# Sums of the unit ahead: when a product with ones is made, and in which bank

## Chip, cores and metric

The kernel runs on one core of a Trainium2 chip. The metric is device time in microseconds (us). The core has five instruction streams: TensorE (PE, matrix products, with its weight loads shown as PEld), VectorE (DVE), ScalarE (ACT), GpSimd (POOL) and SyncE (SP, which here only issues DMAs). Each stream is worked off in the order in which the program wrote it, and streams wait for one another through semaphores. Products land in PSUM, which the program divides into eight banks, each 512 float32 wide on 128 partitions. An ACT or DVE instruction carries the result from there to SBUF.

## What is computed

Four cross-attention layers run one after the other on x (4 batches, 512 query rows, 256 channels), with a context of 1024 rows and 512 channels per batch. Layers 0, 2 and 3 have 16 heads of width 64 and a bias that suppresses some key columns:

```python
q = hidden_states @ Wq            # k = ctx @ Wk, v = ctx @ Wv, split into 16 heads of 64
logits = jnp.einsum('bhqd,bhkd->bhqk', q, k) * scale
logits = logits + col_bias[None, None, :, :]
probs = jax.nn.softmax(logits, axis=-1)
out = jnp.einsum('bhqk,bhkd->bhqd', probs, v)
out = out.transpose(0, 2, 1, 3).reshape(B, HW, HEADS * HEAD_DIM)
out = out @ Wo + bo
out = out + residual
```

Layer 1 has an RMS norm, 16 query heads of width 16 and 4 key heads that each serve 4 query heads ("grouped"). Everything is float32. What matters here is the softmax's denominator: for each query, the sum of exponentials over all 1024 keys.

## The kernel before

**Units and steps.** The work is cut into units of two heads for one batch: 8 units per layer and batch, 96 masked (layers 0, 2, 3) and 32 grouped (layer 1). `order()` lists 96 steps by hand. Each step has one masked unit, `g`, and some also a grouped unit, `lam`. The grouped units stand in four runs of eight steps. `coming` is the grouped unit of the next step. `by_ones` is true where a step has `lam` or `coming`: 36 steps in all. Per run these are an opening step (only `coming`), then eight with a grouped unit, where steps that prepare values (even) and steps that prepare keys (odd) take turns; in the last of them nothing is coming.

**A step** works on `g` and on the unit before it, `g1`. On PE, in the order of the program:

- `scores(g)` (lines 873 and 879): eight tiles of logits, copied by ACT to a buffer (line 883); DVE takes maxima (line 930) and later subtracts them (line 978); ACT takes exponentials (line 984); POOL adds the eight tiles to a running sum `g.acc` (line 1023).
- `attend(g1)` (line 906, 64 output columns): the exponentials of `g1`, finished in the step before, times its values, 16 matmuls.
- then a list `fill` of items, each with a planned duration: `project_out` (line 1112, output projection of two finished units), `project_q` (line 770, evacuated by ACT in line 775), `k_part` (line 556, half a product of keys; after two halves ACT copies in line 561) or `v_pair` (line 609, copied by ACT in line 616), and `attend_grouped`, which calls `attend(lam)` (line 906 with 32 columns) and copies in line 916.
- between them, from a planned time of 12 or 13 us on, `pair(i)`: the logits of the coming grouped unit (line 846, copied by ACT in line 852).

**The planner's clock.** `now` adds up the planned durations of the items. When an item returns a function (its evacuation), `pass_events(now)` first writes out all subtractions and exponentials whose due time lies below `now`, then the evacuation itself. So `now` decides how many exponentials stand ahead of an evacuation on ACT's queue. Due times: the masked unit's exponentials at 3.3 + 1.22 t (t from 0 to 7; in `by_ones` steps t = 7 comes much later), the grouped unit's at 2 t - 7.5 for t from 4 to 7 (0 to 3 stand earlier), and the masked unit's subtractions at 0.7 + 1.2 t.

**The sums.** In the 36 steps the denominators of `g1` come from PE: `sums_beside(g1)` (line 1078) multiplies `g1.acc` by a matrix of ones, two matmuls, into one bank. It returns `turned`, which is put at the head of a list `late`. `late` is worked off before the first `pair`, or at the end of the step where there is none. `turned` transposes the bank's content on DVE (line 809), takes reciprocals, transposes back, gives the bank back, and scales `g1`'s output.

**Banks.** All PSUM space is taken through `Place`. It takes the bank that was given back longest ago by the program's order, among those that are not held. In steps with grouped work (`tabled`), a single bank comes from banks 4 to 7 unless `among` says otherwise, and a double one for scores or logits from a pair of the lower banks:

```python
    if tabled[0]:
        whole = [n for n in whole if n <= last] or whole
    at = min(whole, key=lambda n: max(free[n], free[n + 1]))
elif tabled[0] and any(n in free for n in among):
    at = min((n for n in among if n in free), key=lambda n: free[n])
```

Scores use `last=4`, so they go round (0,1), (2,3), (4,5). `place_out(g1)` takes a single bank for the masked attend and holds it until `turned` is done; `place_out(lam)` takes one for the grouped attend. A bank that is taken again makes PE wait until its former content has been read.

Of the kernel before, what the change touches and what calls it, by code (L numbers as in the profile page):

```python
# [80 lines left out]
def kernel(ctx: ExitStack, tc: tile.TileContext, a: dict, out: bass.AP):  # L81
# [9 lines left out]
    def t_(shape, tag, name, bufs=1, dtype=FP):  # L91
        return sb.tile(shape, dtype, tag=tag, name=name, bufs=bufs)
# [44 lines left out]
    def give_set(g):  # L137
        sets_free.append(g.set)
# [664 lines left out]
    def reciprocal_rows(out_, in_, room):  # L803


        turned = room[:, 0:S]
        short = t_([P, S // 32, 1], "short", f"short{len(turns)}")
        turns.append(0)
        nc.vector.transpose(turned, in_)
        nc.vector.reciprocal(short, turned.rearrange("p (c r) -> p c r", r=32)[:, :, 0:1])  # L810
        nc.vector.transpose(
            out_.rearrange("p (c r) -> p c r", r=32), short.to_broadcast([P, S // 32, 32])
        )
# [78 lines left out]
    def place_out(g, width=1):  # L892
        g.place = Place(width)
        g.po, g.psum = g.place.ap[:, 0:S], g.place.ap[:, S:]

    def attend(g, blocks=range(NT)):
        for t in blocks:
            for j in range(2):
                rows = g.rows[j]
                if not g.masked:  # L900
                    rows = slice(64 * g.h + 32 * j, 64 * g.h + 32 * (j + 1))
                at, first, last = rows, 0, NT - 1
                if not g.masked:
                    at = slice(64 * (t % 2) + 32 * j, 64 * (t % 2) + 32 * (j + 1))
                    first, last = t % 2, NT - 2 + t % 2
                nc.tensor.matmul(  # L906
                    g.po[at, :], lhsT=g.v[:, t, rows], rhs=g.st[t][:, j * S : (j + 1) * S],
                    start=(t == first), stop=(t == last),
                )

    def keep_even(g):


        if g.h == 0:
            gq[g.b, "o"] = t_([P, S], "o1", f"o1_{g.name}")
        nc.scalar.copy(gq[g.b, "o"][64 * g.h : 64 * (g.h + 1), :], g.po[0:64, :])

    def keep_odd(g):
        half = gq[g.b, "o"][64 * g.h : 64 * (g.h + 1), :]
        nc.vector.tensor_tensor(half, half, g.po[64:128, :], ALU.add)  # L920
        if g.h == 0:
            g.place.back()
# [102 lines left out]
    def turn_grouped(g):  # L1025
        normalise_grouped(g, g.place.ap)
        g.place.back()
# [44 lines left out]
        scale_out(g)  # L1072

    def sums_beside(g):
        w = Place(1, among=range(8))
        m = w.ap
        for j in range(2):
            nc.tensor.matmul(  # L1078
                m[g.rows[j], :], lhsT=ones[:, 0:64], rhs=g.acc[:, j * S : (j + 1) * S],
                start=True, stop=True,  # L1080
            )

        def turned():
            g.ot = t_([P, S], "ot", f"ot_{g.name}", bufs=3)
            reciprocal_rows(g.ot, m, g.ot)
            w.back()
            scale_out(g)

        return turned

    def scale_out(g):
        nc.vector.tensor_tensor(g.ot, g.po, g.ot, ALU.mult)
        g.place.back()
# [109 lines left out]
    def head(g):  # L1203
        return steps[step_of[1, g.b, 0]][1]
# [26 lines left out]
    g0, g1 = masked[0:2]  # L1231
# [56 lines left out]
    for n in range(len(steps) + 2):  # L1288
# [4 lines left out]
        g1, attended = attended, g  # L1293
# [62 lines left out]
        late = []  # L1356
# [31 lines left out]
        by_ones = tabled[0]  # L1388
# [44 lines left out]
        def behind(add):  # L1433
            if g is not masked[-1]:
                return add
            late.append(add)

        fill, of_grouped = (
            [
                (1.8 * len(each), lambda each=each: behind(project_out(*each)))  # L1440
                for each in outs if each[0].masked == m
            ]
            for m in (True, False)
        )
# [4 lines left out]
        if fast_k:  # L1449
# [3 lines left out]
            fill = of_keys[:2] + fill + of_keys[2:4] + of_queries + of_keys[4:]  # L1453
        elif fast_v:
            of_values = fast_values(g)
            if fresh:
                of_values[1:4] = of_values[3:4] + of_values[1:3]
                fill = of_values[:2] + fill + of_grouped + of_values[2:4] + of_queries + of_values[4:]
                of_grouped = []
            else:  # L1460
                fill = of_values[:2] + fill + of_queries + of_values[2:]
# [7 lines left out]
        if lam:  # L1469

            def attend_grouped():
                while any(of is lam for _, of, _ in events):
                    events.pop(0)[2]()
                lam.v = head(lam).v
                place_out(lam)
                attend(lam)
                give_set(lam)
                late.append(lambda: keep_odd(lam))
                if lam.h == 1:
                    late.append(lambda: turn_grouped(lam))  # L1480
                return lambda: keep_even(lam)

            total, where = 0.0, 0
            while where < len(fill) and total < (8.0 if by_ones and of_values else 9.5):
                total += fill[where][0]
                where += 1
            fill.insert(where, (3.6, attend_grouped))
            if by_ones:
                fill.insert(where, (1.0, lambda: late.insert(0, sums_beside(g1))))
        elif by_ones:  # L1490
            fill.insert(2, (1.0, lambda: late.insert(0, sums_beside(g1))))
        if soon and soon.first:

            def square():
# [73 lines left out]
```

## Time and profile before

| what | value |
|---|---|
| time, median of 3 runs | 3410.82 us (3410.70 to 3411.05) |
| the profiled execution | 3411.3 us |
| its span (first to last instruction) | 3409.5 us |
| idle time of PE in front of the sums (line 1078) | 0.0 us |
| length of a key step inside a run | 36.5 us |
| length of a value step inside a run | 33.1 us |
| PE's waits on ACT's copies, longest single one | 1.1 us |

The times of the steps are counted from the end of one masked attend to the start of the next on PE's timeline. In the lines of groups, the number behind x counts records, then come busy time, mean time of one record in nanoseconds, and idle time of the engine in front of the group with what ended it. A float32 matmul leaves two records. Matmuls on different columns of the array overlap, so a group's busy time is much less than records times mean. In a timeline, a line stands for a row of instructions of one kind: start, length, engine, line, names, shapes, count, and in brackets the idle time in front of it.

### The profile page before, as it was taken

How to read it: one execution, taken by the hardware profiler on the slowest of the kernel's cores; microseconds unless marked ns; L12 is line 12 of the kernel's file. 1: busy time of each engine (PE TensorE's matmuls, PEld its weight loads, DVE VectorE, ACT ScalarE, POOL GpSimd, SP SyncE). 2: the span in 40 equal slices, each digit the busy share in tenths (PEclk: the TensorE clock that was granted, in tenths of full speed). 3: DMA queues.
4: the chain of work that ended last, by engine and by line, in shares of the span. 5: the costliest groups of instructions: out<-in, count | busy, mean ns of one | idle time of the engine just before them, and what ended most of it. 6: DMA issues, size and time to landing. Idle time of an engine off the chain costs nothing.

```text
span 3409.5 us, 42702 instructions
## 1 busy us (share of the span) xinstructions
PE 3396.9 (100%) x15520; PEld 1654.2 (49%) x15520; DVE 2956.4 (87%) x3872; ACT 2348.4 (69%) x2729; POOL 2596.1 (76%) x1337
## 2 busy tenths in 40 slices
PE   9999999999999999999999999999999999999999
PEld 5555444444444444445455454554444445454554
DVE  7888899988999889988888889888899988889887
ACT  5666688776787768876666666666678776666665
POOL 5888588875888768888668768677588888769775
PEclk9999999999999999999999999999999999999999
DMA  3232111011101120011001110011111101011100
GB/s 109 64 115 85 58 36 52 30 48 38 55 27 30 48 62 30 27 30 55 19 28 53 35 48 30 28 53 56 38 30 52 36 21 53 28 45 52 35 30 10
DMA packets 147733, 151.69 MB, mean 44 GB/s; under 512 B 23608, under 2 KB 125496, under 8 KB 147012
## 3 DMA queue, kind: packets, MB, share of 16 engines
q1 hardware_dynamic: 144958, 140.58, 13.2%
q0 software_dynamic: 2560, 8.39, 0.9%
q8 instruction: 123, 2.02, 0.3%
q14 instruction: 86, 0.70, 0.1%
q10 hardware_dynamic: 6, 0.00, 0.0%
HBM read 132.15 MB, written 15.73 MB: 43 GB/s over the span
## 4 chain that ended last, share of the span: by engine, by line
PE 92%; DVE 5%; ACT 1%; issue 1%; POOL 0%; DMA 0%; DVEq 0%; ACTq 0%; POOLq 0%
PE ps L906 21%; PE ps L669 18%; PE ps L873 18%; PE ps L556 9%; PE ps L609 9%; PE ps L1112 5%; PE ps L770 5%; PE ps L846 4%; DVE ps L890 2%; DVE st L978 1%; PE ps L1078 1%; PE ps L571 1%; ACT st L883 1%; PE ps L879 1%; PE ps L785 0%
## 5 line engine op out<-in xcount | busy, mean ns | idle before, releaser
L1023 POOL TENSOR_TENSOR st<-st 128x1024 f32<-128x1024 f32 x668 | 1581.7, 2368 | 557.1 <-ACT st L984 512.6
L984 ACT ACTIVATE st<-st 128x1024 f32<-128x1024 f32 x1024 | 1042.3, 1060 | 226.8 <-POOL st L976 117.7
L978 DVE TENSOR_TENSOR st<-st,ps 128x1024 f32<-128x1024 f32 x768 | 884.2, 1214 | 3.3
L906 PE MATMUL ps<-st,v 128*64 128x512 f32 (+1 forms) x4064 | 789.8, 595 | 0.0
L976 POOL TENSOR_TENSOR st<-st 128x1024 f32<-128x1024 f32 x256 | 597.8, 2379 | 212.0 <-DVE st L970 106.2
L883 ACT COPY st<-ps 128x1024 f32<-128x1024 f32 x768 | 713.3, 1053 | 55.6 <-PE ps L879 55.4
L890 DVE TENSOR_TENSOR ps<-ps,st 128x1024 f32<-128x1024 f32 x420 | 517.8, 1233 | 210.2 <-ACT st L883 172.1
L930 DVE TRANSPOSE_TENSOR_REDUCE tops<-st 128x32 f32<-128x1024 f32 x544 | 628.3, 1211 | 69.2 <-ACT st L852 64.5
L873 PE MATMUL ps<-qt,kt 64*128 64x512 f32 x3008 | 687.3, 596 | 0.0
L906 PEld LDWEIGHTS ps<-st,v 128*64 128x64 f32 (+1 forms) x4064 | 239.9, 130 | 535.0 <-issue 443.6
L873 PEld LDWEIGHTS ps<-qt,kt 64*128 64x128 f32 x3008 | 280.9, 186 | 345.0 <-ACT st L883 147.5
L609 PE MATMUL ps<-wv,ctx 128*128 128x256 f32 x1344 | 312.1, 385 | 1.1 <-ACT ctx L432 1.1
L669 PE MATMUL ps<-st 128*128 128x128 f32 (+1 forms) x1620 | 308.8, 339 | 2.3 <-ACT ps L692 2.1
L556 PE MATMUL ps<-ctx,wk 128*128 128x512 f32 x672 | 310.9, 604 | 0.0
L609 PEld LDWEIGHTS ps<-wv,ctx 128*128 128x128 f32 x1344 | 250.5, 190 | 92.1 <-issue 54.8
L852 ACT COPY st<-ps 128x1024 f32<-128x1024 f32 x256 | 247.0, 1018 | 62.5 <-PE ps L846 59.0
L669 PEld LDWEIGHTS ps<-st 128*128 128x128 f32 x1620 | 214.6, 192 | 94.2 <-issue 86.7
L684 ACT COPY st<-ps 128x512 f32<-128x512 f32 x45 | 26.3, 585 | 339.2 <-PE ps L669 339.2
L556 PEld LDWEIGHTS ps<-ctx,wk 128*128 128x128 f32 x672 | 121.9, 190 | 180.5 <-issue 163.4
L770 PE MATMUL ps<-x,wq 128*128 128x512 f32 x376 | 180.6, 603 | 2.0 <-ACT x L393 1.1
L1112 PE MATMUL ps<-ot,wo 128*128 128x512 f32 x380 | 173.2, 599 | 0.0
L846 PE MATMUL ps<-qt,kt 32*128 32x512 f32 x1024 | 160.0, 640 | 0.0
(202 smaller groups left out, 2961.6 us busy)
## 6 DMA issues: line engine op xcount, KB each, us to landing
wv<-in_L_xattn_Wv_dram SPq DMA_DIRECT2D x48, 512.0 KB
ctx<-kept SPq DMA_DIRECT2D x24, 1024.0 KB
wk<-in_L_xattn_Wk_dram SPq DMA_DIRECT2D x47, 512.0 KB
wo<-in_L_xattn_Wo_dram SPq DMA_DIRECT2D x96, 128.0 KB
wq<-in_L_xattn_Wq_dram SPq DMA_DIRECT2D x94, 128.0 KB
st<-kept SPq DMA_DIRECT2D x4, 2048.0 KB
qt<-q SPq DMA_DIRECT2D x64, 128.0 KB
kept<-st SPq DMA_DIRECT2D x12, 512.0 KB
```

The source lines that it names most:

```text
L556: nc.tensor.matmul(m, lhsT=g.w["k"][:, k, :], rhs=ctx_half[g.b, n][:, k, :], start=(k == 0), stop=(k == KT - 1),)
L609: nc.tensor.matmul(m[:, half * 2 * P : (half + 1) * 2 * P], lhsT=ctx_half[g.b, t // 4][:, k, t % 4 * P : (t % 4 + 1) * P], rhs=g.w["v2"][: ...
L669: nc.tensor.matmul(m if is_keys else m[:, q], lhsT=right[:, k, :] if is_keys else left_[:, k, q], rhs=left_[:, k, :] if is_keys else right ...
L873: nc.tensor.matmul(m[:, j * S : (j + 1) * S], lhsT=g.kt[g.rows[j], keys], rhs=g.qt[g.rows[j], :], start=True, stop=t > 0,)
L883: nc.scalar.copy(g.st[t], m)
L890: nc.vector.tensor_tensor(top, top, g.st[t], ALU.max)
L906: nc.tensor.matmul(g.po[at, :], lhsT=g.v[:, t, rows], rhs=g.st[t][:, j * S : (j + 1) * S], start=(t == first), stop=(t == last),)
L930: nc.vector.tensor_reduce(out_, of.rearrange("p (b x) -> p b x", x=32), AX.X, op, apply_transpose=True)
L976: nc.gpsimd.tensor_tensor(g.st[t], g.st[t], g.mb, ALU.subtract)
L978: nc.vector.tensor_tensor(g.st[t], g.st[t], g.mb, ALU.subtract)
L984: nc.scalar.activation(st, st, AF.Exp)
L1023: nc.gpsimd.tensor_tensor(g.acc, g.st[0] if t == 1 else g.acc, g.st[t], ALU.add)
```

## The change

Two edits. The bank of the sums is no longer taken from all eight, but as for any single item, from banks 4 to 7. And the item that makes the sums goes to the front of `fill` in all 36 steps; before, it stood directly in front of the grouped attend, or third in the list where the step had no grouped unit. `late.insert(0, ...)` is as it was, so `turned` is still worked off at the same place. In an opening step further items (the grouped queries and values) are put in front of the whole list afterwards, and so in front of the sums.

```diff
     def sums_beside(g):
-        w = Place(1, among=range(8))
+        w = Place(1)
         m = w.ap
         for j in range(2):
             nc.tensor.matmul(
...
             fill.insert(where, (3.6, attend_grouped))
-            if by_ones:
-                fill.insert(where, (1.0, lambda: late.insert(0, sums_beside(g1))))
-        elif by_ones:
-            fill.insert(2, (1.0, lambda: late.insert(0, sums_beside(g1))))
+        if by_ones:
+            fill.insert(0, (1.0, lambda: late.insert(0, sums_beside(g1))))
         if soon and soon.first:
```

## The prediction

> **What bounds the kernel now.** The first view is the page's busy table and its chain of waits. The profiled execution took 3411.3 us, its span is 3409.5 us, and TensorE (PE) is busy all of it. The chain gives PE 92%. So a microsecond that PE stands still is a microsecond on the end, and one that PE does not need is one gained.
>
> ```profile
> PE 3396.9 (100%) x15520; PEld 1654.2 (49%) x15520; DVE 2956.4 (87%) x3872; ACT 2348.4 (69%) x2729; POOL 2596.1 (76%) x1337
> ...
> PE 92%; DVE 5%; ACT 1%; issue 1%; POOL 0%; DMA 0%; DVEq 0%; ACTq 0%; POOLq 0%
> ```
>
> The second view is the groups by line, for the line that is moved: 144 records, 38.9 us in all, and PE never idle in front of it. Two matmuls make four records, so there are 36 products with ones, 1.08 us each.
>
> ```profile
> L1078 PE MATMUL ps<-st,ones 128*64 128x512 f32 x144 | 38.9, 618 | 0.0
> ```
>
> The 36 steps are four batches of nine: an opening step without a grouped unit, then in turn four value steps and four key steps with one. The third view is the timeline, PE and then ACT, of one key step (start, length, engine, line).
>
> ```profile
> 552.75 7.09 PE L906 MATMUL ps<-st,v 128*64 128x512 f32 x32
> 559.77 3.70 PE L1112 MATMUL ps<-ot,wo 128*128 128x512 f32 x8
> 563.30 1.88 PE L770 MATMUL ps<-x,wq 128*128 128x512 f32 x4
> 565.02 5.31 PE L556 MATMUL ps<-ctx,wk 128*128 128x512 f32 x12
> 570.26 1.08 PE L1078 MATMUL ps<-st,ones 128*64 128x512 f32 x4
> 571.27 3.64 PE L906 MATMUL ps<-st,v 128*32 128x512 f32 x32
> ```
> ```profile
> 566.73 2.01 ACT L984 ACTIVATE st<-st 128x1024 f32<-128x1024 f32 x2 [0.33 <-POOL st L976]
> 568.64 0.58 ACT L775 ACTIVATE qt<-ps 128x512 f32<-128x512 f32 x1
> 569.12 3.88 ACT L984 ACTIVATE st<-st 128x1024 f32<-128x1024 f32 x4
> 572.90 0.57 ACT L561 COPY kt<-ps 128x512 f32<-128x512 f32 x1
> ```
>
> PE runs without a hole: masked attend, output projection, query projection, one and a half key products, ones, grouped attend. The copies that empty the banks lag: the query product is done at 565.02 and copied at 569.2, the first key product at about 568.6 and copied at 573.47, 2.2 us **after** the grouped attend began. ACT has exponentials in front of them, which wait for POOL. In the code of before nobody needs these two banks so early.
>
> **The change, part by part.** I count from a, the end of the masked attend (559.77).
>
> *The product itself.* Sixteen rounds of the attend take 7.02 us (552.75 to 559.77), 0.44 a round; two rounds added behind it in the same array form cost 0.88. Today the product takes 571.27 - 570.26 = 1.01. Gain 0.13 a step, where nothing waits. The Trainium skill ("TensorEngine Tiling (Array Packing)", Key Properties) says a change of tiling mode drains the engine; that is a reason for the gain, and the row has its size. Its input, the running sum on POOL, ends 15.3 to 20.1 us before a in all 36 steps (in one value step it ends at 586.03, the attend at 603.27), so no wait there.
>
> *The banks.* Single items take the least recently returned of banks 4 to 7. Scores rotate through (0,1), (2,3), (4,5), so the masked attend's own output and the sums, both taken early now, get 6 and 7 and hold them until the sums are turned on DVE, in the first logits pair. Two banks remain, and by the order of taking: query product 4, first product 5, second product 4 **behind the query copy**, grouped attend's output 5 **behind the first product's copy**. Before, the sums usually lay in 0 or 2, the products in 4 and 5, and the grouped attend took the query's bank.
>
> *The order on ACT.* The item moved to the front adds 1.0 to the clock that releases exponentials, so one more (the third of the masked unit, due at 5.74) goes ahead of the query copy: ten, not nine, in a key step, six, not five, in a value step. Four take 3.88, so 0.97 each: each copy comes 0.97 later.
>
> *Price of a key step.* PE goes on 0.14 us after such a copy: below, ACT's copy ends at 81.13 and PE starts at 81.27.
>
> ```profile
> 80.55 0.58 ACT L692 COPY ps<-ps 128x512 f32<-128x512 f32 x1
> ...
> 81.27 1.95 PE L669 MATMUL ps<-st 128*128 128x512 f32 x4 [0.54 <-ACT ps L692]
> ```
>
> In 12 of the 16 key steps the first key copy ends at a+13.7; new a+13.7+0.97+0.14 = a+14.80 for the grouped attend, against a+11.51: +3.29, 39.5 us. In the other four, behind a value step that holds the grouped unit's output projection (the same timeline at a = 645.14, 1060.62, 1476.09 and 2680.84), it ends at a+12.16: +1.76, 7.0 us. The wait for the query copy (a+9.45+0.97+0.14 against a+9.6 for the second product) lies inside these. Behind the waiting attend stand the logits pairs and the rest of the step; PE has no slack to take it back, so it stays.
>
> *Price of the closing key step* (four, no logits pairs): the sums keep their bank to the end, so the third and fourth key products both take bank 4, each directly behind the copy of the one before.
>
> ```profile
> 743.79 8.85 PE L556 MATMUL ps<-ctx,wk 128*128 128x512 f32 x20
> ...
> 745.82 0.58 ACT L561 COPY kt<-ps 128x512 f32<-128x512 f32 x1 [0.91 <-PE ps L556]
> ```
>
> Twenty records last 8.78 (to 752.57), so the second product's four end at 745.55; its copy ends at 746.40, PE resumes at 746.54: 0.99 each, two per step, 7.9 us.
>
> *Value steps.* The same order of banks, but the copies come sooner. In the tightest kind the first value copy ends at a+7.92:
>
> ```profile
> 688.64 1.98 PE L770 MATMUL ps<-x,wq 128*128 128x512 f32 x4
> ...
> 695.99 0.57 ACT L616 COPY v<-ps 128x512 f32<-128x512 f32 x1
> ...
> 698.48 3.64 PE L906 MATMUL ps<-st,v 128*32 128x512 f32 x32
> ```
>
> With 0.97 and 0.14 that is a+9.03; the grouped attend wants the bank at a+9.84-0.13 = a+9.71. It is covered by 0.68 us; without this cover 10 steps would pay. So 16 times -0.13: -2.1 us. *Opening steps*: the product stands behind the grouped query projections and the small transposes, not behind the attend, in the bank of a query product copied 1.6 us before (393.49 against 395.13): 0.
>
> *Moved along:* DVE adds the output projection one subtract (1.15 us) later, and PE's list of waits has only three for that line, 0.9 us in all, none of them in the 36 steps. No DMA and no POOL instruction moves.
>
> Sum: 39.5 + 7.0 + 7.9 - 2.1 = **+52.3 us** on 3411.3, 3463.6; the profiled execution is 0.5 above the median of 3410.82, so 3463.
>
> **Unknown ends.** The extra exponential: 0 if it fits a hole of ACT, to two of them (1.94) if the tie falls otherwise. Resumption: 0.05 (other rows, PE behind a DVE result) to 0.14. Low: 12 x (13.7+0.05-11.51) + 4 x (12.16+0.05-11.51) + 8 x 0.9 - 2.1 = 34.8, time 3446. High: 16 x 0.97 on top, 67.8, time 3479. I take the middle, since ACT's exponentials run back to back from the query copy on.
>
> The Trainium skill ("TensorE: Matmul & The Clock Gate", Part 1) says PE falls to half its clock after an idle window of about 3.4 us, and regains it after as long a busy one. My longest unbroken idle time is a+12.4 to a+14.8, 2.4 us, under that; the profile's granted clock is full in all 40 slices, with no hole over 1.1 us. By the page, if the gate did close in 12 steps, each would add an estimated 1.7 us, some 20 in all, 3484.
>
> **Rivals.**
> 1. *The banks are free in time*, 3406 (32 x -0.13 = -4.2, 0.12%). This decides if the first key copy ends before a+11.2. For it: PE has no bank wait in these steps today. Against: the copy ends at a+13.7 already. Chance 0.05, and 0.03 for a gain over 0.2% by something I don't see.
> 2. *The waits come, without the later copies*: the extra exponential fills time in which ACT waits for POOL. For: ACT's waits of 1.26 for POOL stand in front. Against: the last one before the query copy is 0.33. 3446, chance 0.15.
> 3. *More is late*: the value steps' 0.68 is eaten, or the clock falls. Each value step that loses one further exponential pays 0.29 plus what follows; with the upper end above, 3479. Chance 0.15.
> Forecast: 0.62.
>
> **Numbers.** A measurement here tells 0.2% (7 us) from nothing. Slower is 0.62 + 0.15 + 0.15 = 0.92, same 0.05, faster 0.03. The range 3446 to 3479 spans the low to the high end.
>
> **What would show it.** After: PE idle in front of the grouped attend, put down to ACT L561, about 2.4 us in 12 key steps, and of the second key product to ACT L775, some 0.9; two waits of about 0.5 to 1 in each closing step; none in value steps; line 1078 at 0.88 a pair. Key steps are 3.3 longer, value steps 0.13 shorter. Wrong if line 906 has no idle time, if the query copy has nine exponentials ahead, or if granted clock dips.

## The result, and the profile after

The changed kernel takes 3468.84 us (median of six runs, 3467.10 to 3472.17), the kernel before in the same comparison 3410.93 us (3410.69 to 3411.14). The ratio is 1.0172, with a 95% interval of 1.0159 to 1.0185: 57.9 us slower. The profiled execution took 3468.61 us with a span of 3466.8 us, 57.3 more than before.

The page of the changed kernel, its busy table, its chain of waits and two of its groups:

```profile
PE 3406.3 (98%) x15520; PEld 1655.1 (48%) x15520; DVE 2956.2 (85%) x3872; ACT 2345.3 (68%) x2729; POOL 2596.0 (75%) x1337
...
PE 82%; POOL 8%; DVE 5%; ACT 5%; issue 1%; DMA 0%; DVEq 0%; ACTq 0%; POOLq 0%
...
L906 PE MATMUL ps<-st,v 128*64 128x512 f32 (+1 forms) x4064 | 798.2, 604 | 34.3 <-ACT kt L561 34.3
...
L556 PE MATMUL ps<-ctx,wk 128*128 128x512 f32 x672 | 315.7, 606 | 14.1 <-ACT qt L775 8.7
```

All engines do the work they did. But PE is no longer the whole end: 10% of the chain has gone over to POOL and ACT, that is to exponentials and to what feeds them, and two PE lines that never stood still now do, for 34.3 and 14.1 us. Before, they read:

```profile
L906 PE MATMUL ps<-st,v 128*64 128x512 f32 (+1 forms) x4064 | 789.8, 595 | 0.0
...
L556 PE MATMUL ps<-ctx,wk 128*128 128x512 f32 x672 | 310.9, 604 | 0.0
```

PE is also busy for 9.4 us more (3406.3 against 3396.9) with the same 15520 instructions; that is a second loss, which idle time does not show. The moved line itself is cheaper, 37.2 us instead of 38.9, and still has nothing in front of it:

```profile
L1078 PE MATMUL ps<-st,ones 128*64 128x512 f32 x144 | 37.2, 595 | 0.0
```

The table of PE's waits in the changed kernel (us in total, times, longest) says who ends them:

```profile
PE ps L906 <- ACT kt L561: 34.3, 16, 2.3
PE ps L556 <- ACT qt L775: 8.7, 12, 0.7
PE ps L556 <- ACT kt L561: 5.4, 8, 0.7
```

Sixteen grouped attends wait for a key copy, twelve second products for the query copy, and eight products in the closing key steps for the key copy before them. The key step shown before, on PE and then on ACT:

```profile
554.74 7.09 PE L906 MATMUL ps<-st,v 128*64 128x512 f32 x32
561.66 1.03 PE L1078 MATMUL ps<-st,ones 128*64 128x512 f32 x4
562.62 3.70 PE L1112 MATMUL ps<-ot,wo 128*128 128x512 f32 x8
566.16 1.88 PE L770 MATMUL ps<-x,wq 128*128 128x512 f32 x4
567.87 3.60 PE L556 MATMUL ps<-ctx,wk 128*128 128x512 f32 x8
572.21 1.98 PE L556 MATMUL ps<-ctx,wk 128*128 128x512 f32 x4 [0.74 <-ACT qt L775]
576.46 5.34 PE L906 MATMUL ps<-st,v 128*32 128x512 f32 x32 [2.27 <-ACT kt L561]
```
```profile
568.72 2.95 ACT L984 ACTIVATE st<-st 128x1024 f32<-128x1024 f32 x3 [0.33 <-POOL st L976]
571.58 0.58 ACT L775 ACTIVATE qt<-ps 128x512 f32<-128x512 f32 x1
572.05 3.88 ACT L984 ACTIVATE st<-st 128x1024 f32<-128x1024 f32 x4
575.84 0.57 ACT L561 COPY kt<-ps 128x512 f32<-128x512 f32 x1
```

The query copy ends at 572.16 and PE goes on at 572.21; the key copy ends at 576.41 and the grouped attend starts at 576.46. Three exponentials, where before there were two, stand in a row in front of the query copy. One thing is new: the grouped attend takes 5.34 us here, and took 3.64 before. The view by windows (start and end, length, busy time of PE, PEld, DVE, ACT and POOL with counts, granted clock, DMA share, GB/s) shows why:

```profile
573.67:577.08 3.41, 1.14 (x10) 0.29 (x12) 3.31 (x6) 3.41 (x5) 3.33 (x2) 1.00 0.00 0
577.08:580.50 3.42, 3.42 (x23) 0.85 (x16) 0.16 (x1) 0.29 (x1) 3.34 (x2) 0.50 0.02 5
580.50:583.91 3.41, 3.41 (x23) 1.08 (x16) 1.40 (x2) 1.53 (x3) 3.25 (x3) 1.00 0.00 0
```

Behind the wait, TensorE's granted clock is at half for 3.41 us. A piece of work that falls wholly into such a stretch gets 1.71 us of its work done and is 1.70 us late. Five of the sixteen waiting attends are hit, at 576, 1006, 1181, 1351 and 2570 us.

Step by step, measured from the end of one masked attend to the next, the 57.3 us come from here (after minus before):

| steps | each | sum |
|---|---|---|
| 12 key steps (the closing ones among them), wait | +3.2 | +38.4 |
| 4 key steps behind an output projection | +1.69 | +6.7 |
| 4 closing key steps, in addition | +1.87 | +7.5 |
| 5 grouped attends at half clock | +1.70 | +8.5 |
| 16 value steps | -0.13 | -2.1 |
| 4 opening steps | -0.20 | -0.8 |
| other steps | | -0.9 |

The sum is 57.3.

### The profile page after: what moved, and what is told of

It reads as the page before. It is cut to its first block, busy times and chain, and to the rows that moved or that the text cites. A ratio compares the mean times of both kernels' runs of the same rounds, so it can differ in the third digit from the quotient of the medians.

```text
span 3466.8 us, 42695 instructions
## 1 busy us (share of the span) xinstructions
PE 3406.3 (98%) x15520; PEld 1655.1 (48%) x15520; DVE 2956.2 (85%) x3872; ACT 2345.3 (68%) x2729; POOL 2596.0 (75%) x1337
## 3 DMA queue, kind: packets, MB, share of 16 engines
q8 instruction: 123, 2.02, 0.2%
## 4 chain that ended last, share of the span: by engine, by line
PE 82%; POOL 8%; DVE 5%; ACT 5%; issue 1%; DMA 0%; DVEq 0%; ACTq 0%; POOLq 0%
PE ps L906 18%; PE ps L669 18%; PE ps L873 17%; PE ps L609 8%; POOL st L976 8%; PE ps L556 6%; PE ps L846 4%; PE ps L770 4%; ACT st L984 3%; PE ps L1112 3%; DVE ps L890 2%; DVE st L978 1%; PE ps L571 1%; PE ps L879 1%; PE ps L1078 1%
## 5 line engine op out<-in xcount | busy, mean ns | idle before, releaser
L906 PE MATMUL ps<-st,v 128*64 128x512 f32 (+1 forms) x4064 | 798.2, 604 | 34.3 <-ACT kt L561 34.3
L556 PE MATMUL ps<-ctx,wk 128*128 128x512 f32 x672 | 315.7, 606 | 14.1 <-ACT qt L775 8.7
```

Source lines behind the costliest of these rows:

```text
L556: nc.tensor.matmul(m, lhsT=g.w["k"][:, k, :], rhs=ctx_half[g.b, n][:, k, :], start=(k == 0), stop=(k == KT - 1),)
L906: nc.tensor.matmul(g.po[at, :], lhsT=g.v[:, t, rows], rhs=g.st[t][:, j * S : (j + 1) * S], start=(t == first), stop=(t == last),)
```

## The experiments

Two questions were open. Which part of the change makes the waits: the place of the matmuls, the range of banks, or the planned duration that lets one exponential more go ahead? And what makes the clock fall after five of the waits and not after the other eleven? All times stand against the kernel before, 3410.7 to 3410.9 us in these comparisons.

**The bank alone.** The kernel before, with one edit; the matmuls stay in front of the grouped attend and ACT's order is that of before.

```diff
-        w = Place(1, among=range(8))
+        w = Place(1)
```

> The sums stay where they were, only their bank is taken from 4 to 7. Theory (banks): at that place they take the query product's bank, so the grouped attend gets the first key product's. It starts 0.05 us after that copy's end: 12 x (13.70 + 0.05 - 11.51) + 4 x (12.16 + 0.05 - 11.51) = 29.7, and the closing steps pay 4 x 1.88 as in the changed kernel, 7.5: 3448 us, plus 1.7 for each grouped attend that runs at a lower clock, up to 3457. No extra exponential, no wait of the second key product. Rival (it is the place in the order that costs): 3411.

Measured: 3457.78 us (3457.65 to 3460.05), ratio 1.0138 (1.0121 to 1.0155). Key steps are longer by 2.24 (one of them by 2.60), those behind an output projection by 0.71, closing ones by a further 1.88. Six attends run at half clock. Its table of waits and PE's timeline of the same key step:

```profile
PE ps L906 <- ACT kt L561: 28.8, 16, 2.5
PE ps L556 <- ACT kt L561: 5.4, 8, 0.7
```
```profile
567.50 5.31 PE L556 MATMUL ps<-ctx,wk 128*128 128x512 f32 x12
572.74 1.08 PE L1078 MATMUL ps<-st,ones 128*64 128x512 f32 x4
575.97 5.34 PE L906 MATMUL ps<-st,v 128*32 128x512 f32 x32 [2.15 <-ACT kt L561]
```

Nothing was moved here, and most of the loss is there all the same, 47 of 58 us. By the order of taking, the sums get the bank that the grouped attend's output had, and the attend gets one behind a key copy. The wait for the query copy is gone, since the second product no longer stands behind it.

**The place alone**, with all eight banks allowed as before. The edit is to the changed kernel.

```diff
-        w = Place(1)
+        w = Place(1, among=range(8))
```

> The sums go to the front, but may take any of the eight banks. Theory (banks): at the front the longest free bank is 6 or 7 anyway, so 32 of the 36 steps get the same banks as in the changed kernel and the time stays at 3469 (3465 to 3473). Rival (the narrower choice of banks is what costs): the wide choice brings the time back to 3406 to 3415.

Measured: 3477.96 us (3477.88 to 3479.87), ratio 1.0197 (1.0180 to 1.0214), slower than the change. In the 32 steps with a grouped unit nothing is better: the bank given back longest ago is one of the upper four at that early point in any case, and the waits are those of the change. The opening steps, where the sums get a lower bank, lose 0.93 to 1.38 each instead of gaining 0.20, through waits that its table newly shows:

```profile
PE ps L556 <- DVE x L1144: 1.9, 2, 0.9
PE ps L1112 <- ACT st L789: 1.4, 4, 0.4
```

Against the change that is 5.5 us, and eight attends instead of five at half clock are 5.1 more in the profiled execution (3479.87); the run was expected at 3469, so the opening steps' part was missed. So either edit by itself is enough to put a product behind a key copy in the key steps. Undoing the move alone brings back 11 of the 58 us, undoing the bank alone nothing.

The program's own takes and returns of banks say the same. Before, the grouped attend's bank is that of the query product in 28 of the 32 steps, and of a value product in four. In the change, in bank alone and in place alone it is one that a key copy has to empty in all 16 key steps.

**The planned duration.** The changed kernel with a duration of nothing for the item, so that ACT's order is that of before.

```diff
-            fill.insert(0, (1.0, lambda: late.insert(0, sums_beside(g1))))
+            fill.insert(0, (0.0, lambda: late.insert(0, sums_beside(g1))))
```

> The changed kernel with a planned cost of 0.0 for the sums, so that no further exponential goes ahead of the key copies in key steps. Theory: each of the 16 key copies comes 0.97 earlier, -15.6: 3453, or 3445 if no grouped attend meets a lower clock. Line 906 waits 12 x 1.3 + 4 x 0.8 by the records' idle time. Rival (the order on ACT plays no part, the bank alone sets the wait): 3469.

Measured: 3455.36 us (3451.94 to 3456.99), ratio 1.0129 (1.0112 to 1.0146). Key steps lose 2.25 instead of 3.2, the four others 0.71 instead of 1.69: the exponential costs 0.95 to 0.98 in every key step. The idle times in front of the attend came out differently from what I had expected, 2.27 and 0.78: with the copies earlier the wait for the query copy is gone, so PE reaches the attend's wait earlier by as much. Six attends fall into half clock.

**Is it the idle time that lowers the clock?** The changed kernel with seven products of ones by ones, in one of the lower banks, in front of the waiting grouped attend of the key steps. The attend starts no earlier; PE only has something to do for part of its wait.

```diff
+                if lam.h == 1:
+                    w = Place(1, among=range(4))
+                    for _ in range(7):
+                        nc.tensor.matmul(w.ap[:, 0:P], lhsT=ones, rhs=ones, start=True, stop=True)
+                    w.back()
                 place_out(lam)
```

> The changed kernel with seven matmuls of ones on ones (128 x 128, result unused) in front of the grouped attend of the key steps, where PE waits some 2.4 us. Theory (PE's idle time lowers the clock): no grouped attend of a key step lasts over 3.1, granted clock 1.00, time 3468.8 - 5 x 1.7 = 3460 (3459 to 3462). Rival (the long grouped attends have another cause, such as a shared port): five of them stay at 4.7 and the time at 3469, or over it if the filling does not fit.

Measured: 3459.84 us (3459.65 to 3460.07), ratio 1.0144 (1.0127 to 1.0161), granted clock full for all of PE's work. PE's timeline there:

```profile
574.01 1.72 PE L1478 MATMUL ps<-ones 128*128 128x128 f32 x14
576.44 3.64 PE L906 MATMUL ps<-st,v 128*32 128x512 f32 x32 [0.71 <-ACT kt L561]
```

Useless work makes the kernel 9.0 us faster than the change, by keeping the clock. The attend starts when it did (576.44 against 576.46) and is back at 3.64 us in all sixteen steps.

**A longer wait.** The changed kernel with one exponential more ahead of the key copies.

```diff
-                pass_events(now)
+                pass_events(now + (0.95 if lam and kk and 9.0 < now < 10.0 else 0.0))
```

> The changed kernel, but with one exponential more in front of the first key copy of the key steps. Theory (the copy sets the wait): +0.97 in each of 16, 15.5: 3484 with five lowered clocks as now; PE then idles 3.2 in one piece and the clock should fall in more of the 12, up to 3496 if in all. Rival (the exponential fits a hole and the copy does not move): 3469.

Measured: 3497.05 us (3494.62 to 3499.59), ratio 1.0252 (1.0236 to 1.0267). The idle time rises to 3.22 us in twelve key steps and 2.70 in four, and 13 of the 16 attends are slowed. Sixteen waits longer by 0.95 make 15.2, and the slowed attends 14 more than in the change, 29 in all, against 28.2 between the medians.

**The rule behind "five of sixteen".** The trace records when the granted clock changes. In the five kernels with lowered clock up to here (the changed one, bank alone, place alone, planned duration, longer wait) all 38 half-clock stretches that end before the program does begin at whole multiples of 3.4133 us from the first of the same trace, to within 0.002 of a multiple, and last 3.413 us, but for one of twice that. So I cut each trace into windows of this grid and added up PE's idle time in each, by the records of its matmuls. All 38 windows in front of a half-clock stretch hold 2.05 us of idle time or more; no other window at full clock holds more than 2.02. The two nearest to the limit are below: a window of the changed kernel with 1.39 us busy, and what followed, and one of the longer wait with 1.37 us busy, and what followed.

```profile
2829.88:2833.30 3.42, 1.39 (x16) 0.49 (x20) 2.90 (x5) 2.94 (x4) 3.34 (x2) 1.00 0.00 0
2833.30:2836.71 3.41, 3.41 (x27) 1.12 (x20) 0.48 (x1) 0.58 (x1) 3.25 (x3) 1.00 0.00 0
```
```profile
1538.92:1542.33 3.41, 1.37 (x4) 0.30 (x2) 3.31 (x6) 3.41 (x4) 3.25 (x3) 1.00 0.00 0
1542.33:1545.74 3.41, 2.76 (x16) 0.78 (x20) 0.49 (x1) 0.60 (x2) 3.33 (x2) 0.50 0.00 0
```

The first leaves the clock at 1.00, the second at 0.50. A wait of 2.27 us lowers the clock if it happens to lie in one window of the grid with 2.05 of its length; where it straddles a border more evenly, it doesn't. Worked out, that is (3.41 + 2.27 - 2 x 2.05) / 3.41 = 0.46 of all positions, 5.6 of twelve; the three kernels with this wait had 5, 6 and 8. A wait of 1.75 can't reach 2.05, and in none of the eight cases did it.

In all these windows the idle time is one piece, so they don't tell a sum from a longest piece. The end of the kernel before does, in one case. Its last matmuls, and the last window with the rest of the span:

```profile
3404.15 1.25 PE L1168 MATMUL ps<-ident,x 128*128 128x128 f32 x8 [0.78 <-DVE x L1130]
```
```profile
3403.43:3406.84 3.41, 1.25 (x8) 0.84 (x8) 1.96 (x3) 0.59 (x1) 0.00 (x0) 1.00 0.13 45
3406.84:3409.50 2.66, 0.00 (x0) 0.00 (x0) 0.00 (x0) 0.00 (x0) 0.00 (x0) 0.50 0.42 139
```

The window holds 2.16 us of idle time in two pieces, 0.72 and 1.44, and the clock falls behind it, where it costs nothing since PE has no work left. Ten of the eleven traces have such a last stretch, each behind a window with 2.16 us of idle time or more.

This rule was read from traces already taken, so it was tried on a new one: two products of ones in place of seven, which leaves a wait of about 1.8 us.

> As busy_wait, with two products of ones by ones in front of the waiting grouped attend in place of seven: the unbroken idle time of TensorE in the 12 key steps falls from 2.27 to about 1.8, the start of the attend and all else stay. In the five traces with lowered clock so far the half-clock stretches begin on a fixed grid of 3.413 us, and follow a window of this grid in which TensorE was idle for 2.05 us or more, and none that had 2.02 or less. Theory (a window of the grid needs over 2.02 idle): no lowered clock in any of the 16 waits, time as busy_wait, 3460. Rival (a wait of this kind closes the gate in some half of the cases, whatever its length between 1.8 and 2.3): 5 or 6 lowered attends at 1.70, 3468.

Measured: 3460.06 us (3459.95 to 3460.13), ratio 1.0145 (1.0128 to 1.0162). The clock stays full for all of PE's work, though the longest unbroken wait is only 0.45 us shorter than that of the change:

```profile
574.24 0.61 PE L1478 MATMUL ps<-ones 128*128 128x128 f32 x4
576.67 3.64 PE L906 MATMUL ps<-st,v 128*32 128x512 f32 x32 [1.82 <-ACT kt L561]
```

**The value steps' share.** The kernel before, with front place and upper banks in the value and opening steps alone.

```diff
-    def sums_beside(g):
-        w = Place(1, among=range(8))
+    def sums_beside(g, wide):
+        w = Place(1, among=range(0 if wide else 4, 8))
...
-                fill.insert(where, (1.0, lambda: late.insert(0, sums_beside(g1))))
+                fill.insert(where if kk else 0, (1.0, lambda: late.insert(0, sums_beside(g1, kk))))
...
-            fill.insert(2, (1.0, lambda: late.insert(0, sums_beside(g1))))
+            fill.insert(0, (1.0, lambda: late.insert(0, sums_beside(g1, False))))
```

> The sums go to the front and to banks 4 to 7 in value and opening steps; key steps as before the change. Theory: 16 x -0.13 and 4 x -0.20 and no wait: 3408.0 us, 0.08% faster than before. Rival (the other banks' order brings waits into the key steps, or nothing is gained): 3411 or more.

Measured: 3407.75 us (3407.64 to 3408.27), ratio 0.9991 (0.9982 to 1.0000). Value steps gain 0.13, opening steps 0.20, and neither line 906 nor line 556 waits for a copy. This part of the change is a small gain.

**The front place without the bank.** The sums hold their bank from the front of the step to the first logits pair. In these two kernels DVE empties it at once, with the first transpose that `turned` did later; reciprocal, second transpose and scaling stay where they were. The second kernel keeps the planned duration of 1.0, and with it the exponential ahead of the copies; the first has 0.0. The cut shows what both change in `sums_beside`.

```diff
+        g.ot = t_([P, S], "ot", f"ot_{g.name}", bufs=3)
+        nc.vector.transpose(g.ot, m)
+        w.back()
+
         def turned():
-            g.ot = t_([P, S], "ot", f"ot_{g.name}", bufs=3)
-            reciprocal_rows(g.ot, m, g.ot)
-            w.back()
+            short = t_([P, S // 32, 1], "short", f"short{len(turns)}")
+            turns.append(0)
+            nc.vector.reciprocal(short, g.ot.rearrange("p (c r) -> p c r", r=32)[:, :, 0:1])
+            nc.vector.transpose(
+                g.ot.rearrange("p (c r) -> p c r", r=32), short.to_broadcast([P, S // 32, 32])
+            )
             scale_out(g)
```

> The changed kernel with the sums in front, but with VectorE's transpose of the sums, which empties their bank, issued directly behind the two matmuls, and a planned cost of nothing; reciprocal, second transpose and scaling stay where they were. Theory: the time goes to the banks and not to the place of the matmuls. The second product then takes the bank of the sums, the grouped attend's output the bank of the query product, and no product stands behind a key copy that TensorE has to wait for: 16 value steps and 16 key steps by -0.13, 4 opening steps by -0.20, sum -4.9, 3406; grouped attend 3.57 in every step, granted clock full. Rival (VectorE is the next to be late: the transpose delays the subtractions of the masked attend's neighbours, by up to 0.75 in each step, and what TensorE waits for with them): not under 3411. Second rival (matmuls in front cost by themselves): 3450 or more.

> As early_transpose, but with the planned cost of 1.0 that the change has, so that the one exponential more stays ahead of the key copies. Theory: an exponential more ahead of the copies costs only where a product of TensorE stands in a bank behind these copies; with the bank free the time is that of early_transpose, 3406 (within 2). Rival (the order on ScalarE costs by itself, 0.97 in each of 16 key steps): 3421.

Measured: 3406.98 us (3406.75 to 3407.35), ratio 0.9989 (0.9980 to 0.9998), and 3406.73 us (3406.61 to 3406.94), ratio 0.9988 (0.9979 to 0.9998). All runs of both lie below all runs of before in the same comparison (3410.53 to 3411.21), so they beat both kernels, if by 4 us only. PE and ACT in the second one, with the extra exponential (line 1119 here is line 1112 of the others):

```profile
558.88 1.03 PE L1078 MATMUL ps<-st,ones 128*64 128x512 f32 x4
559.84 3.70 PE L1119 MATMUL ps<-ot,wo 128*128 128x512 f32 x8
563.38 1.88 PE L770 MATMUL ps<-x,wq 128*128 128x512 f32 x4
565.09 5.31 PE L556 MATMUL ps<-ctx,wk 128*128 128x512 f32 x12
570.34 3.64 PE L906 MATMUL ps<-st,v 128*32 128x512 f32 x32
```
```profile
565.89 2.95 ACT L984 ACTIVATE st<-st 128x1024 f32<-128x1024 f32 x3 [0.33 <-POOL st L976]
568.75 0.57 ACT L775 ACTIVATE qt<-ps 128x512 f32<-128x512 f32 x1
569.23 3.88 ACT L984 ACTIVATE st<-st 128x1024 f32<-128x1024 f32 x4
573.02 0.57 ACT L561 COPY kt<-ps 128x512 f32<-128x512 f32 x1
```

The key copy is as late as in the change: it ends at 573.59, 14.71 us after the start of the sums, where the change has 14.75 (576.41 and 561.66). But PE starts the grouped attend at 570.34 without a hole, since its bank, by the order of taking, is again that of the query product (in all 32 steps of both kernels), copied by 569.32. So a later copy costs nothing by itself, and 0.95 to 0.98 a step where a product of PE stands in its bank. The first rival, that the transpose delays DVE's subtractions at PE's expense, falls with 3407. Key steps gain 0.06 to 0.15, except the same two in both kernels, which lose 0.14 to 0.21; what they lose it to was not followed up.

## Why the prediction was right, and where its size was off

- **The mechanism held in all its places.** Idle time lies where it was said: 16 grouped attends put down to line 561, 12 second products to line 775, two waits in each closing step, none in value steps. The bank-alone and early-transpose runs show that it is the bank, and the planned-duration run shows the exponential's part.
- **Key steps.** Predicted +3.29 and +1.76, measured +3.2 and +1.69. The difference is PE's resumption after a copy: taken as 0.14, the upper of the two ends, it is 0.05 here (copy's end 576.41, attend's start 576.46).
- **Closing key steps.** Predicted two of 0.99, measured +1.87 for both. The extra time is the copy that PE now waits for, as in these lines of the changed kernel's closing step:

```profile
757.94 3.70 PE L556 MATMUL ps<-ctx,wk 128*128 128x512 f32 x8 [0.68 <-ACT kt L561]
762.32 3.70 PE L556 MATMUL ps<-ctx,wk 128*128 128x512 f32 x8 [0.68 <-ACT kt L561]
```

- **Value steps** came out at the predicted -0.13; **opening steps** at -0.20 instead of 0, a part of 0.8 us in all. The pair of line 1078 itself is not at 0.88 as said: from its start to the next item's it is 0.96. The rest of the gain lies in the masked attend's row, 6.92 to the next start instead of 7.02.
- **The exponential** was rightly counted as one, 0.97 (0.95 to 0.98 by the planned-duration run). The rival without it was wrong: three stand in front of the query copy. Its 3446 is what the planned-duration run would give without its clock: 3455.5 in the profiled execution, less 6 x 1.70, is 3445.3.
- **The clock was the mis-sized term.** The step that failed is "My longest unbroken idle time is a+12.4 to a+14.8, 2.4 us, under that", from which I left the clock at full and this term at nothing. The wait was sized well (2.27); five falls of 1.70 us added 8.5 us. A dip of the granted clock was one of the prediction's own three signs of being wrong, and it came; the other two did not. The waits and gains alone come to 57.3 - 8.5 = 48.8, which is under the predicted 52.3; with the clock the time passes it. So part of the closeness is luck: the two errors, -3.5 and +8.5 us, have opposite signs, and it was the waits' places in the grid that made the falls five and not twelve. The trace of before could have warned: at its very end the clock falls behind a window in which PE was still busy for 1.25 us. The Trainium skill ("TensorE: Matmul & The Clock Gate", Part 1) has a window of 3413 ns that runs freely, and these traces agree with it, at 3.4133 us. Its condition for the fall, "≥1 idle window", differs from these traces, in which 2.05 us of idle time in a window was enough. The measurement decides.
- **The rivals.** Banks free in time: wrong by the waits above; it describes the early transpose, which was not the change. "More is late" named two causes in one, the value steps' cover and the clock: the cover of 0.68 us held, the clock did not.

## What to carry to other kernels

Making a result earlier also holds its buffer earlier and longer; ask first who would have got that buffer, and whether the one it gets instead is emptied by an engine with a queue. Where the early place itself is wanted, the first thing to move along is the instruction that empties the bank. And a wait on TensorE should be priced with the clock in mind: here, a wait of over 2 us cost 1.70 us more in about half of its occurrences, and filling part of it with idle products was worth 9 us.

## What was not expected of the hardware

The granted clock falls by a fixed grid of 3.4133 us, not from the start of a wait. At 2.02 us of idle time in a window it stayed full, at 2.05 it went to half for the next window; the limit lies between, near 0.6 of the window. How many waits are hit depends on where they lie in the grid, which shows in the changed kernel's times: one at 3467.10, three from 3468.61 to 3468.97, two at 3472.13 and 3472.17, steps of about one and two times 1.7 us. The mean granted clock of these runs fits, 0.998 for the first, 0.997 for the three and 0.996 for the two. Only the profiled execution's falls were counted, so for the others their number is an inference.

One stretch, in the longer wait, lasted two windows, though PE was idle for only 0.84 us in the first of them. The other 37 half-clock windows in these five kernels held 0.65 us at most, and full clock followed. Where the limit for the return lies, and whether it is one of idle time, stays open.
